# Second cross attention of a perceiver block: 32x32 transpositions on VectorE and a DRAM buffer in place of TensorE transpositions

## The chip, the core and the metric

The kernel runs on one core of a Trainium2 chip. The metric is the device time of one execution in microseconds. Times are the median of several runs; beside them stands one execution that the hardware profiler recorded, and all durations of single instructions come from that execution.

The core's engines work side by side, each through its own list of instructions in order: TensorE (PE in the profile; its weight loads are PEld), VectorE (DVE), ScalarE (ACT), GpSimd (POOL) and SyncE (SP), which here only issues DMAs. Sixteen DMA engines carry the transfers. A matrix product sums over the partitions of its two operands, so that both must have the summed index on the 128 partitions of the on-chip memory; where a tensor has it along a row, it has to be transposed first. That is what this change is about.

## The reference, cut to what matters

Two layers run over 16 batches of 64 latent tokens of width 256; each has a cross attention to a context of 1024 tokens, a self attention and a feed-forward part. The change lies in the second layer's cross attention (8 heads of 64, rotary embedding on the keys). The context is its `x`, the latents its queries; keys and values come from both.

```python
def _L1_xattn_ref(x, latents, gamma_x, beta_x, gamma_l, beta_l, Wq, Wkv, Wo):
    xn = layer_norm(x, gamma_x, beta_x)
    ln = layer_norm(latents, gamma_l, beta_l)
    q = (ln @ Wq).reshape(b, m, h, d)
    kv_x = xn @ Wkv
    k_x, v_x = kv_x[..., :INNER], kv_x[..., INNER:]
    kv_l = ln @ Wkv
    k_l, v_l = kv_l[..., :INNER], kv_l[..., INNER:]
    ...
    k_x = rope_rotate_k(k_x)
    q = jnp.transpose(q, (0, 2, 1, 3)) * scale
    ...
    k = jnp.concatenate([k_x, k_l], axis=2)
    v = jnp.concatenate([v_x, v_l], axis=2)
    attn = jax.nn.softmax(jnp.einsum('bhid,bhjd->bhij', q, k), axis=-1)
    out = jnp.einsum('bhij,bhjd->bhid', attn, v)
    ...
    return out @ Wo
```

## The kernel before

Everything is 32-bit float. The first cross attention fills the first half of the time. It already transposes its probabilities (L593, `x_pb`) and its context (L547, `x_cb`) on VectorE in blocks of 32x32, and carries the blocks to the right partitions with 16 small DMAs from on-chip memory to on-chip memory (`x_pT<-x_pb`, `ctxT<-x_cb`).

The second cross attention (names beginning with `l_`) works in 64 steps `s`, four for each batch. A window `w = s // 2` holds four heads of one batch as two "head halves" `h` of 128 rows (two heads of 64 queries each); two windows make a batch and eight steps a tile of 128 latent tokens. Context comes in half batches `hh` of 512 tokens (`raw[hh]`, four blocks of 128 tokens by 256 features), and each half batch gives two key blocks `kk`, of two 128-row groups of keys each. One step does these things:

- `fetch` loads a half batch ahead (even steps), and `normalise` (L802, ScalarE) brings its tokens to mean 0 and variance 1 in place.
- `turn_context` transposes a quarter: four 128x128 transpositions on TensorE (`l_pt<-ident,l_ctx`) into PSUM, then two evictions by ScalarE (L821, `l_cnT<-l_pt`), which also multiply by the gain of the norm.
- `keys` multiplies the weights by `l_cnT` (`l_pk`), evicts with a bias (L857, `l_kr`), swaps 32-row halves by four DMAs per group (L862, `l_ks<-l_kr`), and joins `kr*cos + ks*sin` (VectorE L865, GpSimd L866, VectorE L867) into `l_kT`, five steps ahead of `s`. Ten buffers hold such key groups.
- `scores` (odd steps) multiplies queries by keys for the next window (`l_s`); `soften` takes the row maximum (L972) and the exponential (L975).
- `turn_probs` divides by the sum (L993) and transposes the 1024 probabilities of 128 rows by eight transpositions on TensorE (`l_ptp<-ident,pr_l`); VectorE and ScalarE copy one half each out of PSUM into `l_pT` (`copy`, L113 and L111).
- `gather` multiplies `raw` by `l_pT` into `l_po`, half of the features in each of two steps; L1036 evicts.

Between these stand pieces of other stages: `values`, `output`, `latents` and `queries` of this attention, the last pieces of the first layer (names `a_`, `f_`) and the self attention of the second (names `s_`), which run along from the third tile on.

TensorE's order is the program's (`pin` keeps it as written). The order on the other engines and in the DMA queue is made by a scheduler before the kernel runs. All DMAs of this stage are issued by SP in its order; a DMA that has to wait holds back those behind it. `bank` is a pool of three PSUM banks that all stages share. A pool's `bufs` says how many tiles of one tag can be in use at once.

Of the kernel before, what the change touches and what calls it, by code (L numbers as in the profile page):

```python
# [8 lines left out]
F32 = mybir.dt.float32  # L9
# [37 lines left out]
def kernel(  # L47
# [713 lines left out]
    with ExitStack() as st:  # L761
        one = st.enter_context(tc.tile_pool(name="l_one", bufs=1))
        two = st.enter_context(tc.tile_pool(name="l_two", bufs=2))
        prp = st.enter_context(tc.tile_pool(name="l_pr", bufs=3))
        kp = st.enter_context(tc.tile_pool(name="l_k", bufs=10))
# [21 lines left out]
        cnT, kT, qT, vlat, pT, pct, oT, probs = ({} for _ in range(8))  # L787
        xn, hT = {}, {}

# [17 lines left out]
        def turn_context(qq):  # L807

            hh, g = divmod(qq, 2)
            if hh >= NHALF:  # L810
                return
            if g == 0:
                cnT[hh] = two.tile([P, NC, 512], F32, tag="cnT", name=f"l_cnT_{hh}")
            pt = bank([P, NC, 2, P], f"l_pt_{qq}")
            for c in range(NC):
                for k in range(2):
                    transpose(
                        pt[:, c, k, :], raw[hh][:, 2 * g + k, c * P : (c + 1) * P], ident
                    )
            for c in range(NC):  # L820
                nc.scalar.activation(  # L821
                    cnT[hh][:, c, g * 256 : (g + 1) * 256],
                    pt[:, c].rearrange("p k t -> p (k t)"), AF.Identity,
                    scale=cols[:, C_GX + c : C_GX + c + 1],
                )
# [15 lines left out]
        def keys(kk):  # L841

            hh, g = divmod(kk, 2)
            if hh >= NHALF:
                return
            b, n = divmod(hh, 2)
            at = slice(n * 512, (n + 1) * 512)
            for i in (2 * g, 2 * g + 1):
                kr2 = kT[b, i, n] = kp.tile([P, 512], F32, tag="kT", name=f"l_kT_{b}_{i}_{n}")
                pk = bank([P, 512], f"l_pk_{kk}_{i}")  # L850
                for c in range(NC):
                    matmul(
                        pk, lhsT=wkv4[:, c, i * P : (i + 1) * P], rhs=cnT[hh][:, c, :],
                        start=(c == 0), stop=(c == NC - 1),
                    )
                kr = two.tile([P, 512], F32, tag="kr", name=f"l_kr_{kk}_{i}")
                nc.scalar.activation(kr, pk, AF.Identity, bias=bkv[:, i : i + 1])  # L857

                ks = two.tile([P, 512], F32, tag="ks", name=f"l_ks_{kk}_{i}")
                for r in range(4):  # L860
                    o = r ^ 1
                    nc.sync.dma_start(  # L862
                        out=ks[32 * r : 32 * r + 32, :], in_=kr[32 * o : 32 * o + 32, :]
                    )
                nc.vector.tensor_tensor(kr2, kr, k4[:, 0, at], ALU.mult)  # L865
                nc.gpsimd.tensor_tensor(ks, ks, k4[:, 1, at], ALU.mult)  # L866
                nc.vector.tensor_tensor(kr2, kr2, ks, ALU.add)  # L867
# [41 lines left out]
        def queries(t):  # L909

            qT[t] = two.tile([P, NPAIR, P], F32, tag="qT", name=f"l_qT_{t}")
# [29 lines left out]
        def scores(w):  # L941
# [11 lines left out]
            for n in range(2):  # L953
                for j in range(2):
                    k = kT.pop((b, 2 * g + j, n))
                    for h in range(2):
                        r = slice(64 * h, 64 * h + 64)
                        matmul(
                            sc[h][64 * j : 64 * j + 64, n * 512 : (n + 1) * 512],
                            lhsT=qT[t][r, 2 * g + j, at], rhs=k[r, :], start=True, stop=True,  # L960
                        )
# [21 lines left out]
        def turn_probs(s):  # L983
# [7 lines left out]
            if h == 0:  # L991
                pT[w] = two.tile([P, NKT, 2, P], F32, tag="pT", name=f"l_pT_{w}")
            nc.vector.tensor_scalar(pr[h], pr[h], inv, None, ALU.mult)  # L993
            nc.vector.tensor_scalar(prl[:, h, :], prl[:, h, :], inv, None, ALU.mult)
            for e in range(2):
                pt = bank([P, 4, P], f"l_ptp_{s}_{e}")
                for k in range(4):
                    kk = 4 * e + k
                    transpose(pt[:, k, :], pr[h][:, kk * P : (kk + 1) * P], ident)
                copy(e, pT[w][:, 4 * e : 4 * e + 4, h, :], pt)  # L1000
# [21 lines left out]
        def gather(w, c):  # L1022
# [6 lines left out]
            for k in range(NKT):  # L1029
                matmul(  # L1030
                    sums[:, c], lhsT=raw[2 * b + k // 4][:, k % 4, f], rhs=pT[w][:, k],
                    start=(k == 0), stop=(k == NKT - 1),
                )
# [65 lines left out]
        def make_self_pieces(t, pool):  # L1099
# [37 lines left out]
            def self_scores():  # L1137
# [13 lines left out]
                for h in range(2):  # L1151
# [3 lines left out]
                    pr = v["pr", h] = tile_of([P, 8, M], f"pr{h}", f"pr{h}")  # L1155
# [71 lines left out]
        for qq in range(2):  # L1227
            turn_context(qq)
        issue_one()
        turn_latents(0)  # L1230
        for qq in range(2, 4):
            turn_context(qq)
        queries(0)
        for qq in range(4, 7):
            normalise(qq)
        keys(0)
        keys(2)
        issue_one()
        scores(0)
        soften(0, 0)  # L1240
        keys(1)
        issue_one()
        turn_context(4)
        turn_context(5)
        keys(3)
        issue_one()
        turn_context(6)
        keys(4)
        issue_one()
        for s in range(NSTEP):  # L1250
# [9 lines left out]
            normalise(s + 7)  # L1260
# [3 lines left out]
            turn_context(s + 7)  # L1264
# [216 lines left out]
def _constants(np):  # L1481
# [21 lines left out]
    k4 = np.concatenate([np.concatenate([a.T, a.T], axis=0) for a in rope(N, 64)], axis=1)  # L1503
# [131 lines left out]
```

## Time and profile before

| | |
|---|---|
| median of 3 runs | 2244.39 us (2239.78 to 2245.81) |
| profiled execution | 2241.03 us, of which its span is 2239.3 us |
| first `l_ptp` (step 0 of the second cross attention) | at 1214 us |
| last `l_pk` | at 1982 us |
| last `l_po` | ends at 2038 us |

The span goes from the first to the last instruction. In a row of a group, the number after the bar is the time in which at least one instruction of the group ran, then the mean length of one in ns; matmuls overlap each other in the array, so that the sum of single lengths is larger than the busy time. After the second bar stands the time for which the engine was idle just before, and what ended it. Two more rows show the work of the second cross attention that remains, on the page:

```profile
L98 PE MATMUL l_pk<-l_cnT,wkv 128*128 128x512 f32 x512 | 232.6, 597 | 3.3 <-ACT l_cnT L821 1.3
L98 PE MATMUL l_po<-l_pT,l_ctx 128*128 128x256 f32 x864 | 199.8, 383 | 0.0
```

### The profile page before, as it was taken

How to read it: one execution, taken by the hardware profiler on the slowest of the kernel's cores; microseconds unless marked ns; L12 is line 12 of the kernel's file. 1: busy time of each engine (PE TensorE's matmuls, PEld its weight loads, DVE VectorE, ACT ScalarE, POOL GpSimd, SP SyncE). 2: the span in 40 equal slices, each digit the busy share in tenths (PEclk: the TensorE clock that was granted, in tenths of full speed). 3: DMA queues.
4: the chain of work that ended last, by engine and by line, in shares of the span. 5: the costliest groups of instructions: out<-in, count | busy, mean ns of one | idle time of the engine just before them, and what ended most of it. 6: DMA issues, size and time to landing. Idle time of an engine off the chain costs nothing. (4 is left out here: it accounts for less than half of the span.)

```text
span 2239.3 us, 32095 instructions
## 1 busy us (share of the span) xinstructions
PE 2144.6 (96%) x11528; PEld 1470.2 (66%) x11528; DVE 1265.6 (57%) x2606; ACT 851.2 (38%) x1633; POOL 310.4 (14%) x302
## 2 busy tenths in 40 slices
PE   7899999999999999999987999999999999998799
PEld 5566666666666666666663656676766666677477
DVE  6755757567475675766526655656565655564311
ACT  2323224333243332333434545555454545443110
POOL 2100001001010010100004222212221212111010
PEclk9999999999999999999989999999999999999799
DMA  7334333343233433443322242222222222112052
GB/s 246 87 96 105 90 76 99 81 105 92 73 100 84 103 91 74 114 108 96 85 78 56 67 140 58 57 58 63 55 63 57 58 57 57 48 48 69 1 170 74
DMA packets 138110, 186.99 MB, mean 84 GB/s; under 512 B 30608, under 2 KB 81296, under 8 KB 137696
## 3 DMA queue, kind: packets, MB, share of 16 engines
q1 hardware_dynamic: 130160, 154.43, 26.6%
q0 software_dynamic: 7792, 30.51, 4.0%
q8 instruction: 92, 1.51, 0.3%
q14 instruction: 66, 0.54, 0.1%
HBM read 67.38 MB, written 1.05 MB: 31 GB/s over the span
## 5 line engine op out<-in xcount | busy, mean ns | idle before, releaser
L98 PE MATMUL x_s<-ctxT,x_qk 128*128 128x512 f32 x1024 | 471.3, 601 | 10.5 <-ACT pr_x L584 10.5
L98 PE MATMUL x_po<-x_pT,ctx 128*128 128x256 f32 x2048 | 459.3, 382 | 4.4 <-DMA x_pT<-x_pb 4.4
L98 PEld LDWEIGHTS x_po<-x_pT,ctx 128*128 128x128 f32 x2048 | 388.6, 191 | 80.4 <-issue 27.0
L98 PEld LDWEIGHTS x_s<-ctxT,x_qk 128*128 128x128 f32 x1024 | 187.1, 190 | 210.0 <-issue 181.5
L577 DVE TENSOR_REDUCE nmax_x<-x_s 128x1 f32<-128x1024 f32 x128 | 156.0, 1218 | 239.0 <-PE x_s L98 238.0
L584 ACT ACTIVATE pr_x<-x_s,shift_x 128x1024 f32<-128x1024 f32 x128 | 142.6, 1114 | 286.8 <-DVE shift_x L581 238.5
L866 POOL TENSOR_TENSOR l_ks<-l_ks,k 128x512 f32<-128x512 f32 x128 | 164.4, 1284 | 578.2 <-DMA l_ks<-l_kr 497.4
L98 PE MATMUL l_pk<-l_cnT,wkv 128*128 128x512 f32 x512 | 232.6, 597 | 3.3 <-ACT l_cnT L821 1.3
L98 PE MATMUL l_po<-l_pT,l_ctx 128*128 128x256 f32 x864 | 199.8, 383 | 0.0
L98 PEld LDWEIGHTS l_po<-l_pT,l_ctx 128*128 128x128 f32 x864 | 161.3, 192 | 21.1 <-issue 0.5
L867 DVE TENSOR_TENSOR l_kT<-l_kT,l_ks 128x512 f32<-128x512 f32 x128 | 89.7, 701 | 147.6 <-POOL l_ks L866 147.0
L98 PEld LDWEIGHTS l_pk<-l_cnT,wkv 128*128 128x128 f32 x512 | 97.6, 192 | 102.2 <-issue 89.5
L593 DVE STREAM_TRANSPOSE x_pb<-pr_x 128x1024 f32<-128x1024 f32 x128 | 157.2, 1236 | 5.9 <-DMA x_pT<-x_pb 2.1
L865 DVE TENSOR_TENSOR l_kT<-l_kr,k 128x512 f32<-128x512 f32 x128 | 89.8, 704 | 98.9 <-ACT l_kr L857 98.2
L857 ACT ACTIVATE l_kr<-l_pk,l_bkv 128x512 f32<-128x512 f32 x128 | 87.7, 685 | 150.7 <-PE l_pk L98 108.9
L618 ACT COPY x_pct<-x_po 128x512 f32<-128x512 f32 x64 | 37.5, 586 | 246.6 <-PE x_po L98 246.6
L178 DVE TENSOR_SCALAR pr_x<-pr_x,inv_x 128x1024 f32<-128x1024 f32 x128 | 100.1, 782 | 3.2
L584 ACT ACT_TABLE_LOAD x42 | 53.9, 1283 | 103.9 <-DVE shift_x L581 103.8
L975 ACT ACTIVATE pr_l<-l_s,nmax_l 128x1024 f32<-128x1024 f32 x64 | 71.3, 1114 | 45.0 <-DVE nmax_l L973 44.6
L102 PEld LDWEIGHTS l_ptp<-ident,pr_l 128*128 128x128 f32 x512 | 57.3, 142 | 41.8 <-issue 18.3
L972 DVE TENSOR_REDUCE nmax_l<-l_s 128x1 f32<-128x1024 f32 x64 | 77.8, 1217 | 7.6 <-PE l_s L98 7.6
L102 PE MATMUL l_ptp<-ident,pr_l 128*128 128x128 f32 x512 | 71.6, 281 | 7.9 <-ACT l_kr L857 4.9
(305 smaller groups left out, 2784.9 us busy)
## 6 DMA issues: line engine op xcount, KB each, us to landing
x_pT<-x_pb SPq DMA_DIRECT2D x1024, 64.0 KB, 2.0
l_ks<-l_kr SPq DMA_DIRECT2D x512, 64.0 KB, 2.0
ctx<-in_context_dram SPq DMA_DIRECT2D x32, 512.0 KB, 5.0
w<-in_m_w_dram POOLq DMA_DIRECT2D x16, 1024.0 KB, 6.3
ctxT<-x_cb SPq DMA_DIRECT2D x240, 64.0 KB, 2.0
l_ctx<-in_context_dram SPq DMA_DIRECT2D x27, 512.0 KB, 4.1
l_ctx_spare<-in_context_dram SPq DMA_DIRECT2D x5, 512.0 KB, 4.2
wq<-in_x_wq_dram POOLq DMA_DIRECT2D x1, 1024.0 KB, 7.4
```

The source lines that it names most:

```text
L98: ins = nc.tensor.matmul(*args, **kwargs)
L102: ins = nc.tensor.transpose(*args, **kwargs)
L178: nc.vector.tensor_scalar(pr, pr, inv, None, ALU.mult)
L577: nc.vector.tensor_reduce(nmax, sc, AX.X, ALU.max, negate=True)
L584: nc.scalar.activation(pr, sc, AF.Exp, bias=shift, scale=1.0, accum_out=total)
L593: nc.vector.transpose(blocks[w][:, :, i], pr.rearrange("p (j k s) -> p j k s", j=4, s=32))
L857: nc.scalar.activation(kr, pk, AF.Identity, bias=bkv[:, i : i + 1])
L865: nc.vector.tensor_tensor(kr2, kr, k4[:, 0, at], ALU.mult)
L866: nc.gpsimd.tensor_tensor(ks, ks, k4[:, 1, at], ALU.mult)
L867: nc.vector.tensor_tensor(kr2, kr2, ks, ALU.add)
L972: nc.vector.tensor_reduce(nmax, sc[h], AX.X, ALU.max, negate=True)
L975: nc.scalar.activation(pr[h], sc[h], AF.Exp, bias=nmax, scale=1.0, accum_out=total[:, 2 * h : 2 * h + 1])
```

## The change

Both transpositions leave TensorE. VectorE transposes 32x32 blocks of the probabilities (`l_pb`) and of the context (`l_cb`); a block then lies in the right place of the wrong partitions. `spread` writes the whole tile to DRAM with one DMA (`l_pd`, `l_cd`) and reads it back with four, in which the partition index and the block index change places. The probabilities of both head halves go together, once per window; the context goes a half batch at a time, beginning with the third; the first two half batches are still transposed by TensorE (`first_context`). The tokens of a half batch then stand in another order in `l_cnT`, and the table of the rotary embedding is permuted to match. The gain moves from the context into the key weights (`wkg`).

To make room, the probabilities have two buffers in place of three, queries one in place of two, the key groups eight named slots in place of ten buffers, and `kr` and `ks` one buffer each that holds both groups of a key block (four swap DMAs of double size per block, in place of eight). The self attention keeps its probabilities in the buffer of its keys. The order of the key blocks before the loop changes, and normalising goes by half batches in odd steps.

```diff
-        prp = st.enter_context(tc.tile_pool(name="l_pr", bufs=3))
-        kp = st.enter_context(tc.tile_pool(name="l_k", bufs=10))
+        prp = st.enter_context(tc.tile_pool(name="l_pr", bufs=2))
+        dram = st.enter_context(tc.tile_pool(name="l_dram", bufs=2, space=bass.MemoryType.DRAM))
+        kp = st.enter_context(tc.tile_pool(name="l_k", bufs=1))
...
+        key_slots = list(range(8))
...
+        def spread(dst, src, name, n):
+
+            d = dram.tile([P, 4, src.shape[2]], F32, tag=name, name=f"{name}_{n}")
+            nc.sync.dma_start(out=d, in_=src)
+            for a in range(4):
+                nc.sync.dma_start(
+                    out=dst[:, a], in_=d[32 * a : 32 * a + 32].rearrange("i j x -> j i x")
+                )
...
+        def turn_context(hh):
+
+            if hh >= NHALF:
+                return
+            dst = context_tile(hh)
+            cb = one.tile([P, 4, NC, 4, 32], F32, tag="cb", name=f"l_cb_{hh}")
+            nc.vector.transpose(
+                cb.rearrange("p j c k s -> p k c j s"),
+                raw[hh].rearrange("p k (c j s) -> p k c j s", c=NC, s=32),
+            )
+            spread(
+                dst.rearrange("p a c k s -> p a (c k s)"), cb.rearrange("p j c k s -> p j (c k s)"),
+                "l_cd", hh,
+            )
...
+            kr = one.tile([P, 2, 512], F32, tag="kr", name=f"l_kr_{kk}")
+
+            ks = one.tile([P, 2, 512], F32, tag="ks", name=f"l_ks_{kk}")
             for i in (2 * g, 2 * g + 1):
...
-                        pk, lhsT=wkv4[:, c, i * P : (i + 1) * P], rhs=cnT[hh][:, c, :],
+                        pk, lhsT=wkg[:, c, i * P : (i + 1) * P],
+                        rhs=cnT[hh][:, :, c].rearrange("p a k s -> p a (k s)"),
...
+                nc.scalar.activation(kr[:, i % 2], pk, AF.Identity, bias=bkv[:, i : i + 1])
+                nc.vector.tensor_tensor(kr2, kr[:, i % 2], k4[:, 0, at], ALU.mult)
+            for r in range(4):
+                o = r ^ 1
+                nc.sync.dma_start(out=ks[32 * r : 32 * r + 32], in_=kr[32 * o : 32 * o + 32])
+            for i in (2 * g, 2 * g + 1):
+                kr2, slot = kT[b, i, n]
+                nc.gpsimd.tensor_tensor(ks[:, i % 2], ks[:, i % 2], k4[:, 1, at], ALU.mult)
+                nc.vector.tensor_tensor(kr2, kr2, ks[:, i % 2], ALU.add)
...
-            qT[t] = two.tile([P, NPAIR, P], F32, tag="qT", name=f"l_qT_{t}")
+            qT[t] = one.tile([P, NPAIR, P], F32, tag="qT", name=f"l_qT_{t}")
...
-            for e in range(2):
-                pt = bank([P, 4, P], f"l_ptp_{s}_{e}")
-                for k in range(4):
-                    kk = 4 * e + k
-                    transpose(pt[:, k, :], pr[h][:, kk * P : (kk + 1) * P], ident)
-                copy(e, pT[w][:, 4 * e : 4 * e + 4, h, :], pt)
+            for n in range(2):
+                nc.vector.transpose(
+                    blocks[w][:, :, h, n],
+                    pr[h][:, n * 512 : (n + 1) * 512].rearrange("p (j k s) -> p j k s", j=4, s=32),
+                )
+            if h == 1:
+                pT[w] = two.tile([P, 4, 2, NKT, 32], F32, tag="pT", name=f"l_pT_{w}")
+                pb = blocks.pop(w).rearrange("p j h n k s -> p j (h n k s)")
+                spread(pT[w].rearrange("p a h k s -> p a (h k s)"), pb, "l_pd", w)
...
-                    sums[:, c], lhsT=raw[2 * b + k // 4][:, k % 4, f], rhs=pT[w][:, k],
+                    sums[:, c], lhsT=raw[2 * b + k // 4][:, k % 4, f],
+                    rhs=pT[w][:, :, :, k, :].rearrange("p a h s -> p h a s"),
...
             keys(s + 5)
-            turn_context(s + 7)
+            if s % 2 == 0:
+                turn_context((s + 6) // 2)
```

## The prediction

> **What bounds the kernel now.** I read the page first, then the table of stretches of time, then the groups of instructions by shape, the timeline of TensorE in a steady stretch, and the rows of the DMAs.
>
> From the page, the busy time of each engine (us, share of the span, instructions):
>
> ```profile
> PE 2144.6 (96%) x11528; PEld 1470.2 (66%) x11528; DVE 1265.6 (57%) x2606; ACT 851.2 (38%) x1633; POOL 310.4 (14%) x302
> ```
>
> An average does not say what the stage of the change costs, so the second view is the table of stretches, cut at the ends of the second cross attention's first loop step (1214) and of its last key work (1985):
>
> ```profile
> core 0: us, PE busy (x) PEld busy (x) DVE busy (x) ACT busy (x) POOL busy (x), PEclk, DMA share, GB/s
> 1160.00:1214.00 54.00, 42.92 (x168) 23.83 (x168) 24.76 (x49) 27.23 (x57) 16.52 (x15) 0.84 0.19 49
> 1214.00:1420.00 206.00, 191.79 (x1067) 127.65 (x1066) 124.39 (x248) 101.61 (x214) 53.09 (x44) 0.98 0.29 80
> 1420.00:1985.00 565.00, 549.05 (x3669) 382.84 (x3667) 321.04 (x640) 284.60 (x580) 122.59 (x99) 1.00 0.22 58
> ```
>
> From 1214 to 1985 TensorE is busy 741 of 771 us (96%) at nearly full clock, VectorE 445 (58%), ScalarE 386 (50%), and the DMA engines a quarter. TensorE's work is what this stage lasts; a microsecond taken from it is a microsecond gained unless something else comes late. What is taken (the page, then the groups by shape; after the bar: busy time of the group in us, mean ns of one, idle time before it):
>
> ```profile
> L102 PE MATMUL l_ptp<-ident,pr_l 128*128 128x128 f32 x512 | 71.6, 281 | 7.9 <-ACT l_kr L857 4.9
> ```
> ```profile
> L547 DVE STREAM_TRANSPOSE x_cb<-ctx 128x512 f32<-128x512 f32 x60 | 40.5, 689 | 0.2
> ...
> L102 PE MATMUL l_pt<-ident,l_ctx 128*128 128x128 f32 x216 | 33.9, 285 | 2.9 <-ACT l_kr L857 2.1 <-DVE a_vm L356 0.8
> ...
> L102 PE MATMUL l_pt<-ident,l_ctx_spare 128*128 128x128 f32 x40 | 6.1, 275 | 0.0
> ```
>
> The busy time of a group counts overlapping matmuls once, so one transposition takes 71.6/512 = 0.14 us of TensorE, not its 281 ns. The timeline of TensorE shows one step of the loop (start, length):
>
> ```profile
> 1554.52 1.95 PE L98 MATMUL l_s<-l_kT,l_qT 64*64 64x512 f32 x16
> 1556.40 1.10 PE L102 MATMUL l_ptp<-ident,pr_l 128*128 128x128 f32 x8
> 1557.33 3.62 PE L98 MATMUL l_po<-l_pT,l_ctx 128*128 128x256 f32 x16
> 1560.79 3.60 PE L98 MATMUL l_pk<-l_cnT,wkv 128*128 128x512 f32 x8
> 1564.22 0.60 PE L102 MATMUL l_pt<-ident,l_ctx_spare 128*128 128x128 f32 x4
> ```
>
> The l_ptp and l_pt rows vanish; scores, gather (l_po) and keys (l_pk) stay.
>
> **Removed from TensorE.** All 512 l_ptp: 71.6 us. Of 256 l_pt, the 16 of the first two half batches stay: 40.0 x 240/256 = 37.5. Sum **109.1 us**. The 10.8 us of idle time before these groups wait mostly for ScalarE's l_kr; I leave them (the wait falls on the next matmul), and count them only in the low end. ScalarE also loses 64 PSUM copies (37.6 us) and most of the l_cnT evictions (53.0), which can only help.
>
> **Same matmuls, other operands.** Keys now read l_cnT in runs of 128, as the first attention's x_s reads ctxT: 460 ns per matmul there (471.3/1024) against 454 (232.6/512): 512 x 6 ns = **+3.1**. The gather reads runs of 32, as x_po does: 459.3/2048 = 224 ns against 231 for l_po: 0.
>
> **VectorE.** Added: 128 transpositions of half a head, at the x_cb row's 689 ns: 88.2 us; 30 of a half batch (128x1024, row x_pb<-pr_x, 1236 ns): 37.1. Gone: the 64 copies L113 l_pT, 43.6. Net +82: 527 of about 670 us, 78%. Free as long as VectorE does not arrive late.
>
> Here a rule of the Trainium skill speaks against the change: "VectorE: DVE Perf Modes", Rules for kernel authors, sends a 128x128 transposition to TensorE if PSUM is an acceptable target, and keeps VectorE's for 32x32. Per head the rows agree with it: 8 x 0.14 = 1.1 us on TensorE against 2 x 0.69 = 1.4 us on VectorE plus two transfers. Priced by engine work alone, the change would lose 125 - 109 = 16 us (2257). But the stretch shows 741 against 445 busy us: the cheaper engine is the full one. I go by the row.
>
> **The new chain: probabilities through DRAM.** The two transpositions of a head pair, one write of 1 MB (l_pd) and four reads of 256 KB (l_pT) now stand between the scores of window w and its first gather. In the changed program's order of instructions VectorE works both heads off right behind the scores: maxima 0.27 + 2 x 1.22 + 0.3; ScalarE's exponential 1.11 and read 0.2 and latents 0.5; then on VectorE l_pct 0.69, scale 0.77, two l_kT sums and two products (2.8), transpositions 2 x 1.38, second scale 0.77, small ones. With their waits the last transposition ends about 12.9 us after the scores. No row shows a transfer to DRAM of this size. Above: a 1024 KB load,
>
> ```profile
> w<-in_m_w_dram POOLq DMA_DIRECT2D x16, 1024.0 KB, 6.3
> ...
> l_ctx<-in_context_dram SPq DMA_DIRECT2D x27, 512.0 KB, 4.1
> ...
> out_dram<-m_res SPq DMA_DIRECT2D x8, 128.0 KB, 1.7
> ```
>
> 6.3 us; the store of out (1.7 for 128 KB) shows that DRAM is no slower to land in. The skill's fit ("SBUF — State Buffer", The DMA setup-cost knee: 2 us + bytes/436e3) gives 4.4. Chain by the rule: 12.9 + 4.4 + 4.4 = 21.7; by the row: **25.5**. I take the row, the low value being undisturbed. The slope of the rows, (6.3-4.1)/512 KB, is 4.4 us per MB; with 0.5 MB ahead of each transfer the chain is 29.9.
>
> What covers it: TensorE's work from the end of scores(w) to gather(w,0): three gathers (3.45), three key blocks (3.6), one scores (2.4) = 23.55 us, plus the other pieces of those steps, from the timeline: 13.0, 13.5, 15.3 and 7.9 us by place in the tile of eight steps (the 13.5, say: l_pvl 1.9, l_out 1.7, s_out 3.5, then latents 0.4 and l_pq, l_pkl, s_pq 6.0), so 31.5 to 38.9 from the third tile on. Covered at 29.9. Shorter windows: at the start, where no self attention runs beside it, 27.4, 27.2 and 23.6; at the end, where no keys are left, 22.4 and 22.2 (there VectorE has 2.8 less to do). Late in sum: 2.7 us at 25.5 (22.7 at the end), 21 at 29.9. I take the middle, **+12**.
>
> **Context through DRAM.** 0.5 MB out and in per half batch, 4.1 + 4.1 us. In the new order the reads of l_cnT stand two steps (some 23 us) ahead of the keys that need them: 0. If that lead is lost, 30 waits of up to 8 us.
>
> **SP's queue.** It takes its DMAs in order. Per two steps before: 16 l_ks at 0.584 and one load at 0.374 us of issue = 9.7 us; after: 8 l_ks of double size, one load, l_pd + 4, l_cd + 4: 8 x 0.584 + 11 x 0.36 = 8.6. But reads of l_pT block it until l_pd has landed, and l_ks of the next keys stand behind them: up to 6.3 us. l_ks feeds GpSimd, then l_kT, needed two or three steps later (over 20 us): 0 on the path.
>
> **Fewer buffers.** kr and ks are now single. Their loop per step: four issues 2.3, landing 2.0, two GpSimd products 2.6, last sum 0.7 = 7.6 us, against a step of (771 - 100)/60, about 11.2. Covered with 3.6 to spare. Eight key slots: those taken were freed by scores at least a gather earlier. Others (probabilities 2, queries 1) are released before they are needed: 0. Prologue: loop of 7.6 per key block against a stretch that is 79% busy already: 0. Gains folded into the weights: two ScalarE instructions.
>
> **Sum**, against the profiled execution (span 2239.3, its time 2241.0): 2241.0 - 109.1 + 3.1 + 12 = **2147 us**. The median of the runs, 2244.4, is 3.4 higher, within the scatter of the runs.
>
> **Rivals.**
> A (0.55), as above: 2147. From 2241.0 - 109.1 - 10.8 + 2.7 = 2124 to 2179, with 1 us of waits in half of the 64 steps added.
> B (0.22): transfers take twice their rows' time because all share the engines: per two steps 4.5 MB (keys 1, probabilities 2, context 1, load 0.5), at 4.4 us per MB 19.8 us of 23. For it: that share. Against it: 58 GB/s at a share of 0.22 means 264 GB/s at full use, 17 us. Chain 12.9 + 25.2 = 38.1 against windows of 31.5 to 38.9: 9.2 us late per tile in six tiles, about 63 in the first two; as windows overlap, a stall in one lengthens the next, so half of 118: 59 in place of 12: 2194.
> C (0.18), slower: the kr/ks loop becomes the bound. Each l_ks waits behind 1.5 MB of probabilities and context (6.6 us): 7.6 + 6.6 = 14.2 us per step. The loop took (2037 - 1214)/64 = 12.9 before: 64 x 1.3 = +83: 2324. It decides above 5.3 us of waiting in every step. For it: one queue, one buffer, SP blocked behind reads. Against it: the order places many l_ks ahead of l_pd.
> D (0.05), no change: VectorE, in order, keeps its waits for GpSimd (147) and l_kr (98): 527 + 245 = 772 us, the old stage: 2241.
>
> **Numbers.** Forecast 2147. A and B together hold 0.77; the range 2120 to 2222 takes in their bounds and some slow way between B and D. Within 0.3% (6.7 us, about what a measurement tells from none): 0.04; faster 0.78; slower 0.18.
>
> **What would show it.** Right: TensorE's busy time falls to about 2039 us, with its share from 1214 on still above 93%; VectorE near 78%; l_pd and l_pT landing in 6 to 8 us; idle time before l_po on DMA l_pT under 25 us, in the first tile and the last. B: over 50 us of such idle time, landings over 10. C: idle time before l_pk or l_s for l_kr or l_kT, and SP waiting for VectorE's l_kT in every step. D: VectorE over 85% busy. Wrong altogether if TensorE's busy time hardly falls.

## The result, and the profile after

The changed kernel takes 2378.5 us (median of 4 runs, 2374.3 to 2383.2); the kernel before, run beside it, 2245.1. The ratio is **1.060** (95% interval 1.057 to 1.063): slower by 133 us where 94 us of gain were forecast (2241.0 to 2147). The profiled execution took 2383.2 us, its span is 2381.4.

The page of the changed kernel: the busy times, then two rows of the 40 slices of the span (in tenths: the clock granted to TensorE, the mean share of the 16 DMA engines).

```profile
PE 2118.3 (89%) x10776; PEld 1428.2 (60%) x10776; DVE 1376.8 (58%) x2708; ACT 763.7 (32%) x1449; POOL 306.4 (13%) x302
...
PEclk8999999999999999999978889899898989898799
DMA  6333343333433334333344655545454545442042
```

The transpositions did leave TensorE (752 matmuls fewer), yet its busy time fell by 26 us only, and it now idles for 263 us of the span (95 before). From slice 21 on the clock granted to TensorE is 0.7 to 0.9 of full speed, and the DMA engines show a share of about one half. The table of stretches of the second cross attention (columns as in the prediction's table; the clock was 0.98 and 1.00 there, the DMA share 0.29 and 0.22):

```profile
1214.00:1420.00 206.00, 141.83 (x597) 84.11 (x598) 118.64 (x220) 64.22 (x135) 41.70 (x35) 0.82 0.51 157
1420.00:2120.00 700.00, 579.36 (x3485) 390.61 (x3484) 434.24 (x771) 248.92 (x499) 133.94 (x112) 0.90 0.50 153
```

TensorE is busy 80% of these 906 us; before it was 96% of 771. VectorE at 61% and ScalarE at 35% are no bound either. The views of waits from 1160 to 2200 (in us, times, longest) say who was late: first for GpSimd, VectorE and ScalarE, then for TensorE.

```profile
POOL l_ks L899 <- DMA l_ks<-l_kr: 580.2, 56, 18.3
DVE l_kT L900 <- POOL l_ks L899: 191.2, 38, 13.0
ACT l_kr L892 <- DMA l_ks<-l_kr: 116.0, 19, 9.5
```
```profile
PE l_po L98 <- DMA l_pT<-l_pd: 61.1, 8, 15.7
PE lnT_s L102 <- ACT l_kr L892: 40.4, 5, 10.0
PE s_po L98 <- ACT s_pT L111: 36.3, 6, 7.7
```

Before, in the same stretch, GpSimd waited 497.4 us for the swaps (it has little else to do), VectorE's l_kT 147.0 for GpSimd, but ScalarE's l_kr only 2.7 us for the swaps, and l_po for nothing. A piece of the chain that ended last (start, length, what):

```profile
1601.24 2.20 SPq L896
1604.75 9.35 DMA l_ks<-l_kr
1614.26 1.28 POOL l_ks L899
1615.56 2.35 DVE l_kT L900 x2
1619.22 4.33 DMA l_ks<-l_kr
```

A swap DMA of 64 KB landed in 2.0 us before; the last one of these, 128 KB, lands after 9.35. ScalarE may not write the single l_kr until it has landed, and what stands behind l_kr on ScalarE (s_pT, lnT's inputs) keeps TensorE. So the loop of the keys lies on this piece of the chain, as rival C had it. It is not the whole chain: from 1214 to 2120 the landings of l_ks make 11.2% of it, those of l_pT 9.0% (the longest 13 to 20 us, between 1237 and 1377), those of l_ctx 8.4%. Open at this point: is it the wait for the data, SP's queue, or the DMA engines?

### The profile page after: what moved, and what is told of

The parts are those of the page before. It is cut to its first block, busy times and chain, and to the rows that moved or that the text cites. A ratio compares the mean times of both kernels' runs of the same rounds, so it can differ in the third digit from the quotient of the medians.

```text
span 2381.4 us, 30082 instructions
## 1 busy us (share of the span) xinstructions
PE 2118.3 (89%) x10776; PEld 1428.2 (60%) x10776; DVE 1376.8 (58%) x2708; ACT 763.7 (32%) x1449; POOL 306.4 (13%) x302
## 4 chain that ended last, share of the span: by engine, by line
PE 65%; DMA 17%; DVE 7%; SPq 4%; ACT 3%; issue 2%; POOL 1%; POOLq 0%; ACTq 0%; DVEq 0%
PE x_po L98 18%; PE x_s L98 17%; PE l_po L98 5%; DMA l_pT<-l_pd 4%; DMA l_ks<-l_kr 4%; DMA l_ctx<-in_context_dram 3%; PE l_pk L98 3%; DMA l_pd<-l_pb 2%; SPq L896 2%; PE x_pa L98 2%; DVE l_kT L900 2%; PE l_s L98 1%; PE s_pq L98 1%; SPq L599 1%; PE m_py L98 1%
## 5 line engine op out<-in xcount | busy, mean ns | idle before, releaser
L98 PE MATMUL x_s<-ctxT,x_qk 128*128 128x512 f32 x1024 | 474.2, 604 | 10.3 <-ACT pr_x L584 10.3
L98 PE MATMUL x_po<-x_pT,ctx 128*128 128x256 f32 x2048 | 457.9, 381 | 4.5 <-DMA x_pT<-x_pb 4.5
L98 PEld LDWEIGHTS x_po<-x_pT,ctx 128*128 128x128 f32 x2048 | 387.6, 191 | 80.1 <-issue 27.1
L98 PEld LDWEIGHTS x_s<-ctxT,x_qk 128*128 128x128 f32 x1024 | 188.1, 192 | 211.7 <-issue 183.8
L98 PE MATMUL l_po<-l_pT,l_ctx 128*128 128x256 f32 x864 | 221.9, 412 | 61.1 <-DMA l_pT<-l_pd 61.1
L98 PEld LDWEIGHTS l_po<-l_pT,l_ctx 128*128 128x128 f32 x864 | 174.1, 207 | 114.5 <-issue 71.7
L900 DVE TENSOR_TENSOR l_kT<-l_kT,l_ks 128x512 f32<-128x512 f32 x128 | 129.1, 1048 | 191.5 <-POOL l_ks L899 191.2
L98 PE MATMUL l_pk<-l_cnT,l_wkg 128*128 128x512 f32 x512 | 233.7, 599 | 6.6 <-DVE a_pr L379 5.6
L98 PEld LDWEIGHTS l_pk<-l_cnT,l_wkg 128*128 128x128 f32 x512 | 97.9, 192 | 107.8 <-issue 93.0
L593 DVE STREAM_TRANSPOSE x_pb<-pr_x 128x1024 f32<-128x1024 f32 x128 | 157.3, 1237 | 5.7 <-DMA x_pT<-x_pb 1.7
L618 ACT COPY x_pct<-x_po 128x512 f32<-128x512 f32 x64 | 37.5, 585 | 245.4 <-PE x_po L98 245.4
L1030 DVE STREAM_TRANSPOSE l_pb<-pr_l 128x512 f32<-128x512 f32 x128 | 84.7, 690 | 0.0
L804 ACT ACTIVATE l_ctx<-l_ctx,cstat 128x256 f32<-128x256 f32 x108 | 57.7, 593 | 70.1 <-DMA l_ctx<-in_context_dram 69.1
```

The costliest lines, as they stand in the source:

```text
L98: ins = nc.tensor.matmul(*args, **kwargs)
L593: nc.vector.transpose(blocks[w][:, :, i], pr.rearrange("p (j k s) -> p j k s", j=4, s=32))
L900: nc.vector.tensor_tensor(kr2, kr2, ks[:, i % 2], ALU.add)
L1030: nc.vector.transpose(blocks[w][:, :, h, n], pr[h][:, n * 512 : (n + 1) * 512].rearrange("p (j k s) -> p j k s", j=4, s=32),)
```

## Experiments

Each diff is against the changed kernel, cut with "...". Times are medians of 2 to 11 runs; in brackets the ratio to the kernel before and its interval. The scheduler orders every kernel anew, so that an edit of one place can change the order on SP, ScalarE and VectorE too; where a comparison rests on an order, it is said how far the two agree (places that differ, out of all).

### Does the loss lie in the transfers?

**no_transfers**: block transpositions on VectorE stay, nothing goes through DRAM; the gathers read one fixed tile of zeros and the keys the first two half batches' context, so the second cross attention's output is not the one asked for.

```diff
+        fixed = two.tile([P, 4, 2, NKT, 32], F32, tag="pT", name="l_pT_fixed")
+        nc.gpsimd.memset(fixed, 0.0)
...
-            dst = context_tile(hh)
+            cnT[hh] = cnT[hh % 2]
...
-            spread(
-                dst.rearrange("p a c k s -> p a (c k s)"), cb.rearrange("p j c k s -> p j (c k s)"),
-                "l_cd", hh,
-            )
...
-                pT[w] = two.tile([P, 4, 2, NKT, 32], F32, tag="pT", name=f"l_pT_{w}")
-                pb = blocks.pop(w).rearrange("p j h n k s -> p j (h n k s)")
-                spread(pT[w].rearrange("p a h k s -> p a (h k s)"), pb, "l_pd", w)
+                pT[w] = fixed
+                del blocks[w]
```

> The changed kernel without its DRAM transfers: VectorE still transposes everything, but nothing is written to DRAM or read back; gather and keys read tiles that stay as they are (so the attention it computes is not the reference's). If the transfers, in whatever way, are the whole loss, the time is the forecast without its waits, 2241 - 109 + 3, so 2120 to 2160 us. If VectorE being late is the loss (rival D and beyond), it stays above 2300.

Measured: **2165.6** (0.965, 0.960 to 0.969). All of the loss is in the transfers, and VectorE with all its transpositions does no harm (TensorE is at 95% of the span): rival D falls. 213 us lie between this kernel and the changed one; what in the transfers costs them is the question of all that follows.

**no_swap** leaves the rotary part of the keys out:

```diff
-            for r in range(4):
-                o = r ^ 1
-                nc.sync.dma_start(out=ks[32 * r : 32 * r + 32], in_=kr[32 * o : 32 * o + 32])
...
-                nc.gpsimd.tensor_tensor(ks[:, i % 2], ks[:, i % 2], k4[:, 1, at], ALU.mult)
+                nc.gpsimd.tensor_tensor(ks[:, i % 2], kr[:, i % 2], k4[:, 1, at], ALU.mult)
```

> The changed kernel with all its DRAM transfers, but without the four swap DMAs per key block (GpSimd multiplies kr itself; the rotary embedding is left out of the keys). Queue theory (rival C: l_ks lands late behind the bulk transfers, and the single kr and ks buffers pass that on to TensorE): most of the 231 us between the forecast and the result comes back, 2150 to 2220 us. Round trip theory (the probabilities themselves come late to the gather): under 80 us come back, above 2300.

Measured: **2303.5** (1.026). Only 75 of the 213 us go with the swaps; 138 stay. By its expectation this spoke for late probabilities. So much it does show: the late swaps are one victim, not the cause.

**swap_on_act** lets ScalarE issue the swaps:

```diff
-                nc.sync.dma_start(out=ks[32 * r : 32 * r + 32], in_=kr[32 * o : 32 * o + 32])
+                nc.scalar.dma_start(out=ks[32 * r : 32 * r + 32], in_=kr[32 * o : 32 * o + 32])
```

> The swap DMAs are issued by ScalarE instead of SyncE, nothing else. If SyncE's order (blocked behind reads that wait, and the 0.6 us per issue) is what makes l_ks late: below 2260 us. If the DMA engines themselves are what l_ks waits for (the bulk bytes are ahead of it in any queue): above 2330. Round trip theory: above 2330 too.

Measured: **2528.4** (1.126). That is above 2330, as for full DMA engines or late data, but far above, with a cost that neither theory had: the issues now stand in ScalarE's queue. The 256 of them take 156 us there in sum (median 601 ns each), about what they take on SP (171 us in the changed kernel, 152 in reads_16 below), and ScalarE's next instructions stand behind them. The run says nothing on SP's queue.

**context_on_pe** keeps the context on TensorE, so that only the probabilities go through DRAM:

```diff
...
-            if s % 2 == 0:
-                turn_context((s + 6) // 2)
+            first_context(s + 7)
```

> Only the probabilities go through DRAM; the context is transposed by TensorE for every half batch, as for the first two. TensorE gets 37.5 us of work back, a third of the bulk bytes goes, and with it the 120 reads of l_cnT whose issues take up to 4 us. Queue theory, if l_cnT is the worst of what l_ks waits behind: 2200 to 2270 us. If l_pd and l_pT are: 2330 to 2400. Round trip theory: 2370 or more, as the probabilities keep their way and TensorE has more to do.

Measured: **2405.3** (1.072), just outside the 2330 to 2400 of l_pd and l_pT as the worst, and inside what late probabilities would give: the context's transfers gone, nothing is won in sum, with 26 to 37.5 us of transpositions back on TensorE. **context_only** is the other half: probabilities on TensorE, context through DRAM.

```diff
...
-            for n in range(2):
-                nc.vector.transpose(
...
+            for e in range(2):
+                pt = bank([P, 4, P], f"l_ptp_{s}_{e}")
+                for k in range(4):
+                    kk = 4 * e + k
+                    transpose(pt[:, k, :], pr[h][:, kk * P : (kk + 1) * P], ident)
...
```

Its transpositions take 128 consecutive columns, which in this kernel's order of keys are not the tokens of one block of 128, so that its output is not the one asked for; the work is the same.

> Probabilities back on TensorE (512 transposes, 71.6 us), the context alone in blocks through DRAM. If the probabilities' trip is the whole loss: 2166 (no transfers) + 71.6 = 2235 to 2250 us, about the kernel before. If the context's trip costs by itself, through the swaps that stand behind its reads: 2260 to 2320 us.

Measured: **2255.0** (1.005, 1.003 to 1.006). The probabilities' trip carries nearly the whole loss; the context's costs some 18 us over 2165.6 + 71.6, by estimate (30 if the transpositions hold TensorE for 59.5 us only, as worked out further down).

### Late data, SP's queue, or the engines?

**unread_transfers**: all transfers stay, nothing waits for what they bring.

```diff
...
-                        rhs=cnT[hh][:, :, c].rearrange("p a k s -> p a (k s)"),
+                        rhs=cnT[hh][:, :, c].rearrange("p a k s -> p a (k s)") if hh < 2 else stand_c[:, :, c],
...
-                    rhs=pT[w][:, :, :, k, :].rearrange("p a h s -> p h a s"),
+                    rhs=stand_p[:, :, :, k, :].rearrange("p a h s -> p h a s"),
```

> Every transfer of the changed kernel stays, to the same tiles, but nothing waits for what it brings: the gathers read the weights wkv as stand-in probabilities and the keys from the third half batch on read wkg as stand-in context, so the second cross attention's output is not the one asked for. Swaps theory (the loss comes from l_ks, which stands behind the bulk transfers on SP's queue and among the 16 DMA engines): nothing of that goes, so 2310 to 2380 us. Lateness theory (the loss is TensorE waiting at l_po and l_pk for data that is still under way): 2170 to 2240 us, near the 2166 without transfers.

Measured: **2392.5** (1.065), above both ranges and nearer to the first. Nothing is gained: with the 61 us before l_po gone, TensorE stands for ScalarE instead (48 us before lnT_s, 30 before s_po). SP's order is another one here, though (155 of 601 places), so the run speaks against the lateness of the round trip as the main cause; that it costs nothing it does not show.

**swap_on_pool** gives the swaps a queue with no bulk in it:

```diff
-                nc.sync.dma_start(out=ks[32 * r : 32 * r + 32], in_=kr[32 * o : 32 * o + 32])
+                nc.gpsimd.dma_start(out=ks[32 * r : 32 * r + 32], in_=kr[32 * o : 32 * o + 32])
```

> The four l_ks DMAs of a step issued by GpSimd, which does nothing in this stage but multiply l_ks and so loses nothing by waiting for it; SP keeps the bulk. Swaps theory in its queue form (l_ks is late because SP issues it late): 2180 to 2290 us. If it is the DMA engines that are full, or if the probabilities are what is late: 2330 to 2400 us.

Measured: **2397.7** (1.068). The page's rows (KB each, median us from issue to landing) for no_transfers and for this kernel:

```profile
l_ks<-l_kr SPq DMA_DIRECT2D x256, 128.0 KB, 2.3
```
```profile
l_ks<-l_kr POOLq DMA_DIRECT2D x256, 128.0 KB, 6.3
```

Alone on its queue a swap still takes 6.3 us, against 2.3 with no transfers beside it, and GpSimd's queue is not what is slow (2.8 in direct_and_loop below). It is not SP's order either. What is left is the place where all queues meet, the 16 DMA engines.

**probs_direct**: 16 DMAs of 64 KB for a window, without DRAM.

```diff
-                pb = blocks.pop(w).rearrange("p j h n k s -> p j (h n k s)")
-                spread(pT[w].rearrange("p a h k s -> p a (h k s)"), pb, "l_pd", w)
+                pb = blocks.pop(w)
+                for a in range(4):
+                    for j in range(4):
+                        nc.sync.dma_start(
+                            out=pT[w][32 * j : 32 * j + 32, a].rearrange("p h k s -> p (h k s)"),
+                            in_=pb[32 * a : 32 * a + 32, j].rearrange("p h n k s -> p (h n k s)"),
+                        )
```

> Probabilities carried straight from the block tile to their partitions by 16 DMAs of 64 KB for a window, as in the first attention, in place of one write and four reads of DRAM; the context keeps its round trip. Lateness theory: one landing of 6 to 9 us goes, and with it the wait of SP for the write; 2240 to 2310 us. Queue theory: 16 issues at 0.5 to 0.6 us take the place of five, SP is held longer; 2380 to 2480 us.

Measured: **2351.5** (1.047), between the two expectations. TensorE now waits 71 us for l_cnT, whose reads stand behind 16 issues.

### A quarter of the engines

The DMA rows in fine slices show what the engines do. In the changed kernel SP issues, around 1716 (timeline of SP):

```profile
1710.42 0.33 SPq L813 DMA_DIRECT2D l_pd<-l_pb  x1
1716.36 2.39 SPq L815 DMA_DIRECT2D l_pT<-l_pd  x4
1719.07 1.42 SPq L815 DMA_DIRECT2D l_cnT<-l_cd  x1
1720.99 4.24 SPq L896 DMA_DIRECT2D l_ks<-l_kr  x4
```

and the DMA view of 1718 to 1723.5, where the four l_pT reads are under way together, shows (the first row in tenths of the mean share of 16 engines, slices of 0.14 us):

```profile
DMA  0112321332232232223132322222331221322232
...
DMA packets 259, 0.52 MB, mean 94 GB/s; under 512 B 6, under 2 KB 6, under 8 KB 259
...
q1 hardware_dynamic: 259, 0.52, 25.2%
```

The share is **25.2%, four engines of sixteen**, at 94 GB/s, for as long as only reads are under way; while l_pd is written (1711 to 1713.8) it is 95.2% and 380 GB/s. The packet records say the same without a mean: from 1720 to 1723 exactly four packets are under way in 85% of the time and never fewer, from 1711 to 1713.5 sixteen in 71%. Four reads in flight together do not raise it: so they share the same four. The read walks its 128 partitions as `"i j x -> j i x"`, 4 blocks of 32 rows: its slowest dimension is 4. This is a rule of the Trainium skill ("DMA: Bandwidth & Descriptors", in the section Why a DMA increments its semaphore by 16 and not by 1): a DMA goes to the largest number of engines up to 16 that divides the slowest dimension of both access patterns, and on SP's queue to the lowest-numbered ones. The 25.2% agrees; that the same four are the lowest-numbered, no run here shows.

What this makes of the stage, as an estimate from these rows: a step takes (2114.5 - 1178.3)/64 = 14.6 us from the first l_ks issue to the last. In two steps, 29.3 us, the reads (1.57 MB at 96 GB/s, between the 94 here and the 98 of 1700 to 1704) take 16.4 us of four engines, which is 4.1 of the mean share's 0.50 x 29.3 = 14.7; the other 10.6 are taken as spread over all. The four engines are then busy 27 of 29.3 us, about nine tenths, the other twelve a third. A mean of one half hid it.

What the four do to a swap stands in the packet records. The four DMAs of a swap are 128 packets of 4 KB. In time order (us):

| swap issued | first 96 packets start | last 32 packets start |
|---|---|---|
| changed kernel, 1720.99 to 1725.23 | 1723.99 to 1726.50 | 1731.92 to 1734.28 |
| changed kernel, 1900.55 to 1904.38 | 1901.79 to 1905.60 | 1911.59 to 1913.91 |
| reads_16 (below), 1716.75 to 1719.17 | 1717.91 to 1719.72 | 1719.83 to 1720.33 |

Twelve sixteenths of the swap go as they are issued. The other four sixteenths go when the reads are through: the last 2 KB packet of l_pT ends at 1731.70, the 97th packet of the swap starts at 1731.92. Of the 13 swaps between 1420 and 2100 whose packets can be told from those of l_cd, 12 have such a gap, of 3.4 to 6.5 us; in reads_16 none of 22 has more than 0.16.

**reads_16** cuts the same reads the other way: by destination block, 32 partitions of four rows, slowest dimension 32. Bytes, rows, number of DMAs and the DRAM buffer stay.

```diff
-            for a in range(4):
-                nc.sync.dma_start(
-                    out=dst[:, a], in_=d[32 * a : 32 * a + 32].rearrange("i j x -> j i x")
-                )
+            for j in range(4):
+                nc.sync.dma_start(
+                    out=dst[32 * j : 32 * j + 32],
+                    in_=d[:, j].rearrange("(a i) x -> i a x", a=4),
+                )
```

> The four reads of a round trip cut by destination block j (32 partitions x 4 rows of 2 KB or 1 KB) in place of by source block a (128 rows, walked as 4 x 32): the same bytes, rows and number of DMAs, the same DRAM buffer. In the trace the reads by a run at a DMA share of 0.2 and 98 GB/s for 3.5 to 6.5 us on end, as if on 4 of the 16 engines. Engines theory (every l_ks, l_ctx and write has a share on those four engines and waits behind the reads there): the loss goes, 2160 to 2210 us, DMA share without long stretches of 0.2. Volume theory (100 MB more through the engines delay the swaps whatever their form): 2320 to 2390 us.

Measured: **2274.3** (1.012, 1.010 to 1.014): 104 us are won back, and volume alone is not the cause; 109 us above no_transfers stay, so the forecast of 2160 to 2210 is missed as well. SP's order is another one, too (282 of 601 places differ from the changed kernel), so the 104 us are not the form's alone. The DMA view of 1722 to 1726, again reads, of l_cnT and l_pT:

```profile
...
q1 hardware_dynamic: 599, 0.90, 93.1%
```

The engines' share in the reads goes from 25.2% to 93.1%.

Then only one of the two tensors is cut by j (for reads_16_probs; with `"l_cd"` for reads_16_context):

```diff
+            if name == "l_pd":
+                for j in range(4):
...
+            else:
+                for a in range(4):
```

> Only the probabilities' reads cut by j, the context's stay by a. Engines theory: of the two reads' 15 us of four engines in two steps, 10 go; the context's 5 us left cost about what they cost beside TensorE's transposes (2255 - 2238 = 17 us), so 2180 to 2240 us. Volume theory: 2320 to 2390 us.

> Only the context's reads cut by j. Engines theory: the probabilities' 10 us of four engines in two steps stay, beside l_ks and l_ctx; 2280 to 2360 us. Volume theory: 2320 to 2390 us, which this run alone does not tell apart; together with the other two it does.

Measured: **2419.8** and **2394.6**, both above the changed kernel and above every range given for them. The reason shows in the waits of reads_16_probs:

```profile
PE l_pk L98 <- DMA l_cnT<-l_cd: 167.3, 21, 10.3
```

The scheduler planned SP's order anew in each of these kernels. In the changed kernel's piece above the reads stand between l_pd and the next swaps; in reads_16_probs (timeline of SP) behind them, and SP waits there for VectorE's l_kT first:

```profile
1720.15 0.38 SPq L813 DMA_DIRECT2D l_pd<-l_pb  x1
1731.90 2.42 SPq L903 DMA_DIRECT2D l_ks<-l_kr  x4
1734.43 2.28 SPq L822 DMA_DIRECT2D l_cnT<-l_cd  x4
1737.15 2.35 SPq L816 DMA_DIRECT2D l_pT<-l_pd  x4
```

So each differs from the changed kernel in two things. But reads_16 has the order of reads_16_probs (timeline of SP):

```profile
1706.70 0.38 SPq L813 DMA_DIRECT2D l_pd<-l_pb  x1
1716.75 2.42 SPq L897 DMA_DIRECT2D l_ks<-l_kr  x4
1719.27 1.97 SPq L815 DMA_DIRECT2D l_cnT<-l_cd  x4
1721.33 1.80 SPq L815 DMA_DIRECT2D l_pT<-l_pd  x4
```

Only 20 of 601 places of SP's order differ between the two (46 of 758 on ScalarE, 120 of 1238 on VectorE). What they compare is the form of the context's reads: 2419.8 against 2274.3, **145 us**. In this order the swaps go ahead of the reads and have no late quarter (no gap above 0.15 us in 21 swaps); here the slow read itself is late, and TensorE waits 167.3 us for it, against 29.1 in reads_16.

The next set takes the swaps out of SP's order (GpSimd issues them), with swap_on_pool as its base; both kinds of read are cut in reads_16_pool.

> Both reads cut by j, and the l_ks DMAs issued by GpSimd, so that on SP nothing but bulk is left and no read stands behind a swap that waits. Beside swap_on_pool (2398, the same with reads by a). Engines theory with SP's order as the rest of the loss: 2170 to 2230 us, better than the kernel before. If what is left of the loss in reads_16 is the volume: 2260 to 2290 us.

> As reads_16_pool, but the context's reads stay cut by a. Engines theory: the context's 5 us of four engines in two steps cost 17 us beside TensorE's transposes; 2190 to 2260 us. If the half that is cut by a alone brings back the whole loss even with SP's order alike, the engines theory in this form falls: 2350 to 2400 us.

> As reads_16_pool, but the probabilities' reads stay cut by a (SP's order is that of swap_on_pool). Engines theory: the 10 us of four engines in two steps stay; 2280 to 2360 us. By the other theory 2380 to 2400 us.

| swaps on GpSimd, reads cut by j | us | against 2397.7 |
|---|---|---|
| none (swap_on_pool) | 2397.7 | |
| context | 2371.8 | -25.9 |
| probabilities | 2293.5 | -104.2 |
| both (reads_16_pool) | 2267.7 (1.010, 1.008 to 1.013) | -130.0 |

Between the first two rows the order of every engine is the same but for 2 to 5 places, so the 25.9 are the form of the context's reads alone. In the other two rows the writes and reads keep their order among themselves (all but 2 to 4 places); loads and context writes stand elsewhere (43 and 62 of 345 places of SP in all). The parts add up (25.9 + 104.2 = 130.1; the runs of reads_16_pool scatter by 15 us): the form of the reads is worth about 130 of the 232 us between swap_on_pool and no_transfers. Two of the three expectations missed: 2371.8 and 2293.5 lie between the ranges of their theories, so that the form counts, but for less than was thought. A swap lands in 3.4 us (page of reads_16_pool) in place of 6.3:

```profile
l_ks<-l_kr POOLq DMA_DIRECT2D x256, 128.0 KB, 3.4
l_pd<-l_pb SPq DMA_DIRECT2D x32, 1024.0 KB, 3.9
l_pT<-l_pd SPq DMA_DIRECT2D x128, 256.0 KB, 5.4
```

Reads_16_pool did not reach its 2170 to 2230, though; it lies where its expectation put the volume.

### What stays of the loss

**reads_16_unread** is reads_16 with the two edits of unread_transfers.

> reads_16 with stand-ins as in unread_transfers (gathers read wkv, keys from the third half batch on read wkg: the output is not the one asked for). If what is left in reads_16 is TensorE waiting for l_cnT and l_pT that were issued behind a swap: 2170 to 2220 us. If it is SP's, GpSimd's and ScalarE's loop around l_ks: 2250 to 2280 us.

Measured: **2327.5**, outside both ranges and slower than reads_16, which waits for its data. SP's order is the same (18 of 601 places differ), but those of ScalarE and VectorE are not (255 of 758, 458 of 1238), and SP stands 512 us at l_ks for VectorE's l_kT there, 365 in reads_16. Whether the order makes the 53 us is open, and so is what late data costs in reads_16.

**reads_16_no_swap** is reads_16 with the edits of no_swap.

> reads_16 without the l_ks DMAs: GpSimd multiplies l_kr itself by the sine, so the rotary part of the keys is left out. If the l_ks loop is what is left: 2170 to 2200 us, close to the 2166 without transfers. If the rest lies with the round trips themselves (late data, SP blocked): 2240 to 2270 us.

Measured: **2227.0** (0.992, 0.989 to 0.994), between its two ranges: of what stays, 41 us (against reads_16_pool) to 47 (against reads_16) go with the swaps. 61 us stay between it and no_transfers; TensorE's busy time accounts for 14 (2078.3 against 2063.9), the rest is idle time that no run here assigns (25 us of it before l_po, for l_pT).

**no_dram_for_context** is reads_16_pool with the edit of context_on_pe and a second l_kr:

```diff
-            kr = one.tile([P, 2, 512], F32, tag="kr", name=f"l_kr_{kk}")
+            kr = two.tile([P, 2, 512], F32, tag="kr", name=f"l_kr_{kk}")
```

> Context back on TensorE (240 transposes, about 34 us), probabilities through DRAM with reads by j, swaps on GpSimd, and l_kr twice in the place that the context's block tile frees, so that ScalarE can write the next keys while the swaps of the last are under way. 1 MB of 4.5 per two steps goes. Engines and loop theory: 2166 + 34 plus at most 40 for the loop, 2200 to 2240 us, below the kernel before. If the bulk of the probabilities alone is enough to hold the loop: 2250 to 2280 us.

Measured: **2275.1** (1.013, 1.010 to 1.015). Context on TensorE and a second l_kr gave nothing over reads_16_pool in sum; what they won, if anything, the context's transpositions took again (TensorE is busy 2115.7 us against 2094.9). A second l_kr alone was not run.

**direct_and_loop** is the same kernel with the edit of probs_direct in place of the round trip.

> As no_dram_for_context, but the probabilities go straight from the block tile to their partitions by 16 DMAs of 64 KB (1 MB for a window in place of 2, no DRAM). Engines and loop theory: less bulk beside the swaps, 2195 to 2230 us, the fastest of all with transfers. If 16 issues on SP (9.4 us of a window) or the number of DMAs is the limit: 2250 us or more.

Measured: **2238.3** (0.9965, 0.9954 to 0.9976; the kernel before beside it 2245.7). Its expectation ended at 2230. It beats both kernels, the one before by 7 us only, just above what can be told from no change. With 1 MB for a window in place of 2 and none of the reads that ran on four engines, TensorE's clock is 0.95 (1214 to 1420) and 0.99 (1420 to 2000), and l_po waits 5.9 us for l_pT.

## Why the prediction was wrong, step by step

- **The step that failed** is the cost of the transfers. The terms "with 0.5 MB ahead of each transfer", "4.4 us per MB" and "Each l_ks waits behind 1.5 MB of probabilities and context (6.6 us)" all price a byte on the whole of the engines. The reads run on four: 1 MB takes 1.05 MB / 94 GB/s = 11 us, not 6.3, and what matters more, the quarter of a swap that lies on those four waits behind it there. The order of the read's dimensions stood in the diff; the prediction weighed a transfer's size and its setup cost, and left its shape out. This is about 130 of the 232 us (the table). With it mended the change would still have lost: 2267.7 and 2274.3 are above the kernel before. Of that rest, 41 to 47 us go with the swaps, whose loop was put at nothing as well; some 60 no run assigns.
- **"up to 6.3 us. l_ks feeds GpSimd, then l_kT, needed two or three steps later (over 20 us): 0 on the path"**: wrong in both halves. The landing of l_ks, 4 to 12 us in the chain, decided, not its place behind SP's wait (swap_on_pool changed nothing). And l_ks has to land sooner than l_kT is needed: ScalarE writes l_kr again in the next step, because kr is single, and waited 116 us for it.
- **"Covered with 3.6 to spare" (kr and ks single)**: the loop of 7.6 us was sized with a landing of 2.0. With the 9.35 of the chain above it is 15 us, against a step of 14.6 that was measured. With free transfers (no_transfers) ScalarE's l_kr waits 12.9 us for it in all, so this term was right for its landing time.
- **Rival C** had the mechanism and, with 2324, the side; it was given 0.18. Its wait of 6.6 us was near the measured lengthening (9.35 - 2.0 = 7.4 in the piece of chain above), though for another reason than bytes; that its 2324 came near is in part luck. Its argument against itself, "the order places many l_ks ahead of l_pd", looked at SP's queue, while the waiting was at the engines.
- **Chain through DRAM, +12 late**: late data exists (61 us before l_po, where 12 were expected), but leaving out the wait won nothing (unread_transfers, with another order). Once the reads use 16 engines, the write lands in 3.9 us and a read in 5.4 (reads_16_pool), below the 6.3 taken.
- **Context: 0.** Its trip costs 18 to 30 us (context_only, against an estimate); its reads' form alone 26 (the table), and 145 in the order of reads_16.
- **TensorE: -109.1.** Mis-sized. no_transfers shows the gain when nothing disturbs it: TensorE's busy time 2144.6 to 2063.9, 80.7 us, and 79 us in time. The groups' busy times overlap their neighbours': in the timeline shown in the prediction l_ptp starts at 1556.40 and l_po at 1557.33, so eight transpositions hold the array for 0.93 us, not 1.10; four l_pt start at 1564.22 and hold it for 0.44, not 0.60, as the row behind them in that view shows (`1564.66 1.88 PE L98 MATMUL l_pvl<-wkv,hT_l 128*128 128x512 f32 x4`). 64 x 0.93 + 60 x 0.44 = 86. A forecast of 2147 was thus out of reach by some 20 us even with free transfers.
- **VectorE, +82 and free**: +111 us of busy time, and free, as no_transfers shows: priced by engine work alone the change came out at 2257, and without its transfers it took 2165.6. The rule that sends such transpositions to TensorE did not decide here.
- **Signs.** TensorE's busy time near 2039 and its share above 93%: no (2118, 80%). VectorE near 78%: no, 61% of a longer stage. Over 50 us before l_po (B's sign): yes, and it misled. C's signs came in part: SP waited for l_kT 91 us, but 27 times in 64 steps; the idle time for l_kr was ScalarE's own (116 us) and TensorE's before lnT_s (40) and s_pk (7), hardly before l_pk or l_s.

## What to carry to other kernels

Before a DMA is priced by its bytes, read its access patterns: a slowest dimension of 4 put these transfers on four engines, and a trace shows it as a share of 0.25 with nothing else under way, while the mean over the stage looks half empty. A transfer off the critical path can still lengthen one that shares its engines (a swap that takes 2.3 us alone took 6.3), so price the shortest loop that has a DMA in it (here a single buffer's 7.6 us) with landings under load. And where a scheduler orders a queue, compare variants only where the orders agree: cutting one of two reads was slower than cutting none, until the swaps were out of that queue, and the kernels whose orders agreed gave the cleanest numbers.

## What the runs showed of the hardware that was not expected

Where TensorE waited more, the granted clock was lower and its matmuls were slower. With the same 10776 matmuls TensorE is busy 2063.9 us at a mean clock of 0.980 (no_transfers) and 2118.3 at 0.938 (the changed kernel): 54 of the 215 us between their spans are busy time. The row of l_po in the page of the changed kernel:

```profile
L98 PE MATMUL l_po<-l_pT,l_ctx 128*128 128x256 f32 x864 | 221.9, 412 | 61.1 <-DMA l_pT<-l_pd 61.1
```

412 ns for a matmul that took 383 before (and 388 in no_transfers, where it multiplies zeros). The loss is not spread over all matmuls: l_pk, which hardly waits in the changed kernel (6.6 us), takes 599 ns against 597 before. In reads_16 it is the other way round:

```profile
L98 PE MATMUL l_pk<-l_cnT,l_wkg 128*128 128x512 f32 x512 | 249.5, 633 | 52.6 <-DMA l_cnT<-l_cd 29.1
```

There l_pk waits 52.6 us and takes 633 ns, and l_po (9.3 us) 390. In both runs the slow matmuls are in the group with the waits. Whether idle time lowers the clock, or something else that goes with it, no run here tells apart.
